# A selective scan with its products moved off VectorE: B in transposed layout on ScalarE, C on GpSimd, the sum over states by TensorE transposes

## The chip, the core and the metric

The kernel runs on one core of one Trainium2 chip. A core has a matrix engine (TensorE, PE; its weight loads are listed apart as PEld), three engines for elementwise work (VectorE, DVE; ScalarE, ACT; GpSimd, POOL), a queue engine that issues transfers (SyncE, SP), an on-chip memory of 128 partitions (SBUF) and a small accumulator memory of eight banks of 128 x 512 float32 (PSUM), which TensorE writes and which GpSimd is not used on here. Each engine runs its own list of instructions in order, and semaphores make one engine wait for another. The metric is the device time of one execution in microseconds; lower is better.

## What is computed

The input is x of shape 4 x 32 x 32 x 256: 4 batches of 1024 tokens with 256 channels. Everything is float32. Layer 0 is a convolution with a selective scan, layer 1 an attention and a mixture of 16 experts. The change touches layer 0 alone:

```python
x = _layernorm(src, ln1_g, ln1_b) @ w_in + b_in           # 256 -> Dn = 512 channels
x = gelu(depthwise_conv3x3(x) + conv_b).reshape(B, L, Dn)  # L = 1024 tokens
dt_raw, Bm, Cm = split(x @ w_x, [R, R + N])                # R = 16, N = 64 states
dt = softplus(dt_raw @ w_dt + dt_bias)
A = -exp(A_log)                                            # Dn x N
def step(h, inp):                                          # h: B x Dn x N
    dA = exp(dtt[:, :, None] * A)
    h = dA * h + (dtt * xt)[:, :, None] * Bt[:, None, :]
    y = einsum('bdn,bn->bd', h, Ct)
...
y = ys + x * D_skip
out = _layernorm(y, ln2_g, ln2_b) @ w_out + b_out
return src + out
```

For each of 4 batches, 512 channels and 64 states there is a recurrence over 1024 tokens. Its input is dt x B, its decay is exp(dt A), and what it gives is multiplied by C and summed over the 64 states.

## The kernel before

The program is written in Python that unrolls all loops. A tile framework takes the instructions that the Python code traces, orders them for each engine by a priority list of its own, gives out buffers from pools (`bufs=3` means three buffers that are used in turn) and puts in the semaphores. So the order on an engine is not always that of the source, and a tile can only be written when the last reader of the buffer's earlier content is done.

The residual stream `t_all` stays in SBUF, tokens on partitions. Layer 0 goes batch by batch (`for b in range(NB)`). The 512 channels are held as DK = 4 blocks of 128 partitions, and tokens run along the free dimension, in NHALF = 2 halves of 512 (one PSUM bank).

- Front part (L184 to L265): layernorm of the tokens, transposes (`transposed`, L107), the projection in (L201), the convolution as nine products with diagonal matrices (L214), gelu, the projection to B, C and dt (L229, L234; B and C stand in `bct`, states on partitions, tokens along the row), and the softplus in steps on ScalarE, VectorE and GpSimd (L247 to L265), which gives `dt` and `dtx` = dt x. Its tiles z, e, ln and u have two buffers each.
- Scan part (L275 to L331): for each half of the tokens and each of the 64 states n. `drive` (L288) spreads row n of B over all partitions with a product (L282), ScalarE copies it to SBUF as `bb` (L292), and VectorE and GpSimd each multiply two of the four blocks of `dtx` with it (L295), which gives `dbx`. ScalarE makes the decay `da` in PSUM (L307), VectorE runs the scan of each block (L310), 512 tokens in one instruction. Row n of C is spread into PSUM as `p_c`, VectorE multiplies the four blocks of h with it in one instruction (L318), and TensorE adds the product `hc` into four banks `y`, channels on partitions, by multiplying with the identity (L322). The last column of h is kept in `last` as the start of the second half.
- Rear part (L327 to L371): y + D x (L328), layernorm over the channels by means of products with a matrix of 1/512 (L341, L349), the projection out (L365) and the residual sum (L370, L371).

Layer 1 (attention, router, experts; lines from 373 on) is the same before and after. A float32 product is two passes on TensorE, a transpose one.

Of the kernel before, what the change touches and what calls it, by code (L numbers as in the profile page):

```python
# [18 lines left out]
def over_middle(ap, n):  # L19
    """[P, F] read n times: [P, n, F]."""  # L20
    return ap.unsqueeze(1).to_broadcast([ap.shape[0], n, ap.shape[1]])


def over_last(ap, n):
    """[P, F] with each element read n times: [P, F, n]."""
    return ap.unsqueeze(2).to_broadcast([ap.shape[0], ap.shape[1], n])
# [3 lines left out]
def conv_ssm_attn_moe_kernel(ctx: ExitStack, tc: tile.TileContext, a: dict, out: bass.AP):  # L30
# [24 lines left out]
    # The residual stream, tokens on partitions: token (g * 128 + p) is t_all[p, g].  # L55
# [14 lines left out]
    def load_rows(name, k, n, pool):  # L70
        """A [k * 128, n] matrix, rows on partitions."""
        t = pool.tile([P, k, n], F32, name=name.lower() + "_sb")
        nc.sync.dma_start(out=t, in_=a[name].rearrange("(k p) n -> p k n", p=P))
        return t

    def load_column(name, k, pool, lo=0):
        """A vector along partitions, in k blocks of 128."""
        t = pool.tile([P, k], F32, name=f"{name.lower()}_col")
        with nc.allow_non_contiguous_dma(reason="small vectors, once"):
            nc.scalar.dma_start(  # L80
                out=t, in_=a[name][lo : lo + k * P].rearrange("(k p) -> p k", p=P)
            )
        return t

    def load_bcast(name, n, pool):
        """A vector along the free dimension, on all partitions."""
# [4 lines left out]
    def token_layernorm(pool, dst, src, n, tag):  # L91
        """dst = (src - mean) / sqrt(var + 1e-5) over the last dimension of [P, n, C]."""
# [14 lines left out]
    def transposed(psum, src, n, evacuate, tag):  # L107
        """[P tokens, n, C] -> evacuate(ck, half, [P channels, 512 tokens] in PSUM)."""
# [14 lines left out]
    # ------------------------------------------------------------------  # L123
    # Layer 0: conv + selective scan, channels on partitions
    # ------------------------------------------------------------------
    with ExitStack() as l0:
# [28 lines left out]
        # One diagonal matrix for each tap and channel block: the depthwise conv on TensorE.  # L155
# [6 lines left out]
        # 1 / DN everywhere: a product with it is the mean over channels, on all partitions.  # L162
        avg = w0.tile([P, P], F32, name="avg")
        nc.vector.memset(avg, 1.0 / DN)
        # The padded conv inputs; their borders stay zero.
# [6 lines left out]
        acts = l0.enter_context(tc.tile_pool(name="acts0", bufs=1))  # L172

        for b in range(NB):
# [3 lines left out]
            dtx = acts.tile([P, DK, L], F32, name="dtx")  # L178
            bct = acts.tile([P, L], F32, name="bct")

            with tc.tile_pool(name=f"ps_a{b}", bufs=4, space=PSUM) as ps_a, tc.tile_pool(
                name=f"pre{b}", bufs=1
            ) as pre:
                xn = pre.tile([P, NT, C], F32, name="xn")  # L184
                token_layernorm(pre, xn, tb, NT, "ln1")
                xT = pre.tile([P, CK, L], F32, name="xT")

                def put_x(ck, half, ps):
                    nc.scalar.activation(
                        xT[:, ck, blk(half)], ps, AF.Identity,  # L190
                        bias=b1[:, ck : ck + 1], scale=g1[:, ck : ck + 1],
                    )

                transposed(ps_a, xn, NT, put_x, "ps")

                for m in range(DK):
                    pad = pads[m % 2]
                    for half in range(NHALF):
                        ps = ps_a.tile([P, BANK], F32, name="ps_in", tag="ps")
                        for ck in range(CK):  # L200
                            nc.tensor.matmul(  # L201
                                ps, w_in[:, ck, blk(m, P)], xT[:, ck, blk(half)],
                                start=(ck == 0), stop=(ck == CK - 1),
                            )
                        nc.vector.tensor_scalar(  # L205
                            pad[:, 1 + half * ROWS : 1 + (half + 1) * ROWS, 1 : 1 + WW],
                            ps.rearrange("p (h w) -> p h w", w=WW),
                            b_in[:, m : m + 1], None, ALU.add,
                        )
                    for half in range(NHALF):  # L210
                        ps = ps_a.tile([P, BANK], F32, name="ps_conv", tag="psc", bufs=2)
                        for k in range(9):
                            i, j = divmod(k, 3)
                            nc.tensor.matmul(  # L214
                                ps.rearrange("p (h w) -> p h w", w=WW),
                                diag[:, m, k, :],
                                pad[:, half * ROWS + i : (half + 1) * ROWS + i, j : j + WW],
                                start=(k == 0), stop=(k == 8),
                            )
                        nc.scalar.activation(  # L220
                            xg[:, m, blk(half)], ps, AF.Gelu_apprx_tanh, bias=cb[:, m : m + 1]
                        )

                dtr = pre.tile([R, L], F32, name="dtr")
                for half in range(NHALF):
                    psb = ps_a.tile([P, BANK], F32, name="ps_bc", tag="ps")
                    psd = ps_a.tile([P, BANK], F32, name="ps_dtr", tag="ps")
                    for m in range(DK):
                        nc.tensor.matmul(  # L229
                            psb, w_x[:, m, R:], xg[:, m, blk(half)],  # L230
                            start=(m == 0), stop=(m == DK - 1),
                        )
                    for m in range(DK):
                        nc.tensor.matmul(  # L234
                            psd[:R, :], w_x[:, m, :R], xg[:, m, blk(half)],
                            start=(m == 0), stop=(m == DK - 1),
                        )
                    nc.scalar.copy(dtr[:, blk(half)], psd[:R, :])
                    nc.vector.tensor_copy(bct[:, blk(half)], psb)

                # softplus(z) = max(z, 0) + log1p(e), e = exp(-|z|). With u = fl(1 + e),
                # log1p(e) = ln(u) + (e - (u - 1)) to within a rounding.
                for m in range(DK):
                    z = pre.tile([P, L], F32, name="z", tag="z", bufs=2)
                    for half in range(NHALF):
                        ps = ps_a.tile([P, BANK], F32, name="ps_dt", tag="ps")
                        nc.tensor.matmul(  # L247
                            ps, w_dt[:, blk(m, P)], dtr[:, blk(half)], start=True, stop=True
                        )
                        nc.vector.tensor_scalar(  # L250
                            z[:, blk(half)], ps, dtb[:, m : m + 1], None, ALU.add
                        )
                    e = pre.tile([P, L], F32, name="e", tag="e", bufs=2)
                    nc.scalar.activation(e, z, AF.Abs)
                    nc.scalar.activation(e, e, AF.Exp, scale=-1.0)
                    ln = pre.tile([P, L], F32, name="ln", tag="ln", bufs=2)
                    nc.scalar.activation(ln, e, AF.Ln, bias=1.0)
                    u = pre.tile([P, L], F32, name="u", tag="u", bufs=2)
                    nc.vector.tensor_scalar(u, e, 1.0, 1.0, ALU.add, ALU.subtract)
                    nc.gpsimd.tensor_tensor(u, e, u, ALU.subtract)  # L260
                    nc.gpsimd.tensor_tensor(u, u, ln, ALU.add)
                    nc.vector.scalar_tensor_tensor(
                        dt[:, m, :], z, 0.0, u, ALU.max, ALU.add
                    )
                    nc.gpsimd.tensor_tensor(dtx[:, m, :], dt[:, m, :], xg[:, m, :], ALU.mult)  # L265

            # h[d, n, t] = exp(dt[d, t] A[d, n]) h[d, n, t - 1] + dt[d, t] x[d, t] B[n, t];
            # y[d, t] = sum over n of h[d, n, t] C[n, t]: d on partitions, t along the scan.
            # TensorE copies the rows of B and C to all partitions and adds up over n.
            yt = dt  # L270
            last = acts.tile([P, NS, DK], F32, name="last")
            with tc.tile_pool(name=f"ps_y{b}", bufs=1, space=PSUM) as ps_y, tc.tile_pool(
                name=f"ps_e{b}", bufs=2, space=PSUM
            ) as ps_e, tc.tile_pool(name=f"scan{b}", bufs=2) as scanp:
                for seg in range(NHALF):  # L275
                    y = [
                        ps_y.tile([P, BANK], F32, name=f"y{m}", tag=f"y{m}") for m in range(DK)
# [372 lines left out]
```

## Time and profile before

| what | value |
|---|---|
| time, median of 3 runs | 7884.99 us (7884.57 to 7887.02) |
| span of the profiled execution | 7886.5 us |
| batch 0: first scan to last C product | 164.8 to 1196.1 us |
| batch 1 | 1383.7 to 2414.9 us |
| batch 2 | 2602.6 to 3633.7 us |
| batch 3 | 3821.0 to 4852.5 us |
| layer 1 | from about 4897 us on |
| busy: PE / DVE / ACT / POOL | 6606.9 / 5134.6 / 2326.0 / 1381.8 us |

The profiled execution's time is its span, as nothing lies around it that the runs' times would show. In the rows of a profile, "L310 DVE TENSOR_TENSOR_SCAN h<-da,dbx 128x512" is an instruction of line 310 on VectorE that writes tile h from da and dbx; behind it stand the count, the busy time in all, the mean of one in ns, and behind the bar the idle time of the engine just before such instructions, with what ended it. In timeline rows the first two numbers are start and length in us; rows of equal instructions that follow each other are merged, with their count. Instructions that follow each other without a gap overlap a little in these records, so the step from one start to the next is the better measure of a steady cost.

### The profile page before, as it was taken

The page shows a single profiled execution, that of the slowest core. Times are in us where ns is not written, and L with a number is a line of the kernel's source. Part 1 is how long each engine was busy: PE and PEld are TensorE (multiplying, and loading weights), DVE is VectorE, ACT ScalarE, POOL GpSimd, SP SyncE. Part 2 cuts the span into 40 slices and gives each one's busy share as a digit, 9 for nine tenths or more (in the row PEclk, how much of TensorE's full clock was granted, in tenths as well). Part 3 has the DMA queues.
Part 4 walks back from the last instruction along what each step waited for, and adds up shares of the span by engine and source line. Part 5 has one row for each costly group of instructions (what it writes and reads, how often), then busy time and mean ns, then how long its engine had stood idle before and what let it go on. Part 6 is the DMA issues. An engine that isn't in the chain of part 4 may idle for free.

```text
span 7886.5 us, 46169 instructions
## 1 busy us (share of the span) xinstructions
PE 6606.9 (84%) x16768; PEld 3257.8 (41%) x16768; DVE 5134.6 (65%) x5222; ACT 2326.0 (29%) x3771; POOL 1381.8 (18%) x631
## 2 busy tenths in 40 slices
PE   6777777777778677777777777999999999999999
PEld 2222323222233222323232233655555555555555
DVE  3999993999994899995799999542222222222222
ACT  2444442444442444442444443211111111111111
POOL 2222221322220423221322221000000000000000
PEclk8999998899999899999899999889999999999999
DMA  1000000000000000000000000000000000000000
GB/s 30 0 0 0 0 0 0 0 0 0 0 0 0 0 0 0 0 0 0 0 0 0 0 0 24 1 0 8 8 16 8 8 8 8 16 8 8 8 8 22
DMA packets 37701, 39.78 MB, mean 5 GB/s; under 512 B 10704, under 2 KB 28624, under 8 KB 37472
## 3 DMA queue, kind: packets, MB, share of 16 engines
q1 hardware_dynamic: 28240, 36.13, 1.5%
q8 instruction: 131, 2.15, 0.1%
q10 hardware_dynamic: 9232, 0.70, 0.1%
q14 instruction: 98, 0.80, 0.0%
HBM read 32.63 MB, written 4.19 MB: 5 GB/s over the span
## 4 chain that ended last, share of the span: by engine, by line
DVE 45%; PE 43%; issue 9%; POOL 1%; ACT 1%; DMA 0%; ACTq 0%; SPq 0%; DVEq 0%; POOLq 0%
DVE h L310 26%; PE p L591 22%; PE pf L602 11%; DVE hc L318 10%; DVE dbx L295 8%; PE ps_conv L214 3%; PE po L365 1%; PE ps_in L201 1%; PE ps_t L113 1%; PE pqk L426 1%; PE pkv L474 0%; PE y L322 0%; POOL u L260 0%; PE ps_dtr L234 0%; PE ps_bc L229 0%
## 5 line engine op out<-in xcount | busy, mean ns | idle before, releaser
L322 PE MATMUL y<-hc,ident 128*128 128x512 f32 x4096 | 2106.8, 663 | 12.8 <-DVE hc L318 12.8
L307 ACT ACTIVATE da<-dt,l_conv_a_log_sb 128x512 f32<-128x512 f32 x2048 | 1415.1, 691 | 2025.9 <-DVE h L310 2012.0
L591 PE MATMUL p<-xfT,w 128*128 128x512 f32 x4096 | 1781.0, 593 | 0.3 <-DVE pr L539 0.3
L295 POOL TENSOR_TENSOR dbx<-dtx,bb 128x1024 f32<-128x1024 f32 x512 | 1217.8, 2379 | 2825.6 <-DVE h L310 2820.5
L282 PE MATMUL p_c<-bct,ident 128*128 128x512 f32 x1024 | 630.0, 700 | 997.2 <-DVE hc L318 997.1
L322 PEld LDWEIGHTS y<-hc,ident 128*128 128x128 f32 x4096 | 884.1, 216 | 1198.1 <-issue 1179.0
L597 DVE TENSOR_TENSOR hT<-s,p 128x512 f32<-128x512 f32 x512 | 352.0, 688 | 1437.3 <-PE p L591 1436.6
L310 DVE TENSOR_TENSOR_SCAN h<-da,last,dbx 128x512 f32<-128x512 f32 x1024 | 1264.8, 1287 | 0.0
L310 DVE TENSOR_TENSOR_SCAN h<-da,dbx 128x512 f32<-128x512 f32 x1024 | 1193.4, 1207 | 0.1
L318 DVE TENSOR_TENSOR hc<-h,p_c 128x2048 f32<-128x2048 f32 x512 | 1169.8, 2285 | 28.1 <-DVE h L310 1.8
L591 PEld LDWEIGHTS p<-xfT,w 128*128 128x128 f32 x4096 | 778.9, 190 | 926.7 <-issue 919.8
L596 ACT ACTIVATE s<-p 128x512 f32<-128x512 f32 x512 | 305.7, 597 | 2324.3 <-PE p L591 2324.3
L602 PE MATMUL pf<-w,hT 128*128 128x256 f32 x4096 | 904.9, 379 | 0.0
L602 PEld LDWEIGHTS pf<-w,hT 128*128 128x128 f32 x4096 | 778.2, 190 | 160.4 <-issue 61.2
L282 PEld LDWEIGHTS p_c<-bct,ident 128*128 128x128 f32 x1024 | 156.7, 191 | 1422.2 <-DVE hc L318 1412.0
L282 PE MATMUL p_b<-bct,ident 128*128 128x512 f32 x1024 | 549.7, 619 | 143.1 <-ACT bb L292 92.4
L606 DVE SCALAR_TENSOR_TENSOR t_all<-pf,disp,t_all 128x256 f32<-128x256 f32 x512 | 247.8, 484 | 601.3 <-PE pf L602 601.3
L295 DVE TENSOR_TENSOR dbx<-dtx,bb 128x1024 f32<-128x1024 f32 x512 | 634.8, 1240 | 3.1 <-ACT bb L292 3.1
L292 ACT COPY bb<-p_b 128x512 f32<-128x512 f32 x512 | 299.5, 585 | 294.7 <-DVE dbx L295 246.4
L282 PEld LDWEIGHTS p_b<-bct,ident 128*128 128x128 f32 x1024 | 195.6, 194 | 417.5 <-ACT bb L292 246.0
L214 PE MATMUL ps_conv<-pad,diag 128*128 128x512 f32 x576 | 249.8, 592 | 0.0
L205 DVE TENSOR_SCALAR pad<-ps_in,l_conv_b_in_col 128x512 f32<-128x512 f32 x32 | 24.1, 753 | 229.9 <-PE ps_in L201 229.8
(143 smaller groups left out, 2077.9 us busy)
## 6 DMA issues: line engine op xcount, KB each, us to landing
w<-in_L_ffn_w_dram SPq DMA_DIRECT2D x48, 512.0 KB, 3.9
t_all<-in_x_dram SPq DMA_DIRECT2D x4, 1024.0 KB, 7.6
out_dram<-t_all SPq DMA_DIRECT2D x8, 512.0 KB, 2.9
l_attn_w_qkv_sb<-in_L_attn_W_qkv_dram SPq DMA_DIRECT2D x1, 768.0 KB, 6.6
l_conv_w_in_sb<-in_L_conv_w_in_dram SPq DMA_DIRECT2D x1, 512.0 KB, 11.4
l_conv_w_out_sb<-in_L_conv_w_out_dram SPq DMA_DIRECT2D x1, 512.0 KB, 7.4
l_attn_b_qkv_row<-in_L_attn_b_qkv_dram ACTq DMA_DIRECT2D x1, 384.0 KB, 5.3
l_conv_w_x_sb<-in_L_conv_w_x_dram SPq DMA_DIRECT2D x1, 288.0 KB, 9.9
```

The costliest lines, as they stand in the source:

```text
L214: nc.tensor.matmul(ps.rearrange("p (h w) -> p h w", w=WW), diag[:, m, k, :], pad[:, half * ROWS + i : (half + 1) * ROWS + i, j : j + WW], ...
L282: nc.tensor.matmul(ps, ident[:, row : row + 1].to_broadcast([P, P]), bct[:, blk(seg)], start=True, stop=True,)
L292: nc.scalar.copy(bb, pb)
L295: eng.tensor_tensor(dbx[:, lo:hi, :], dtx[:, lo:hi, blk(seg)], over_middle(bb, hi - lo), ALU.mult,)
L307: nc.scalar.activation(da, dt[:, m, blk(seg)], AF.Exp, scale=A[:, m, n : n + 1])
L310: nc.vector.tensor_tensor_scan(h[:, m, :], da, dbx[:, m, :], 0.0 if seg == 0 else last[:, n, m : m + 1], ALU.mult, ALU.add,)
L318: nc.vector.tensor_tensor(hc, h, over_middle(pc, DK), ALU.mult)
L322: nc.tensor.matmul(y[m], ident, hc[:, m, :], start=(n == 0), stop=(n == NS - 1))
L591: nc.tensor.matmul(ps, w[:, ck, blk(hk, P)], xfT[:, ck, blk(tbk)], start=(ck == 0), stop=(ck == CK - 1),)
L596: nc.scalar.activation(s, p1, AF.Silu)
L597: nc.vector.tensor_tensor(hT[:, hk, :], s, p2, ALU.mult)
L602: nc.tensor.matmul(pf, hT[:, hk, blk(j, P)], w3[:, hk, :], start=(hk == 0), stop=(hk == HK - 1),)
```

## The change

In the scan, four things are laid out in another way.

1. **dt x B.** `dtx` is transposed once a batch on TensorE, into `dtxT` with tokens on partitions and channels along the row, and so is B, into `bT`. For a state n, B is then one number per partition, and ScalarE multiplies a token tile of 128 tokens x 512 channels with it as the `scale` of an activation (L323, four a state). TensorE transposes the 16 blocks of 128 x 128 back into PSUM (L330), from where the scan reads them. The decay `da` now goes to SBUF (L332, four buffers).
2. **C.** The C rows are written to a scratch tensor `cd` in the device memory once a batch (L245), and for each state one row is loaded onto all 128 partitions (L318, three buffers). GpSimd multiplies h with it, two blocks at a time (L346). It also makes the copies into `last` (L344).
3. **The sum over n.** Instead of adding up `hc` with channels on partitions, `turned_sum` (L304) adds transposes of its 128 x 128 blocks into the four banks `y`, which now have tokens on partitions. Their first summand is the transpose of D x, for which GpSimd multiplies `xg` with D in place (L294).
4. **After the sum,** the second layernorm works on tokens on partitions with VectorE's statistics instructions (L357 to L363), and its result is transposed back for the projection out. This now runs after each half, before the scans of the next half in VectorE's order.

VectorE keeps the scans and has neither product any more. All pools of layer 0 are opened once rather than once a batch; the tiles of the front part have one buffer each and share them with others (z with xn, e with xT, bct with ln, dtx with u). PSUM is four banks for `y` and four that everything else takes in turn (`bank()`).

```diff
         acts = l0.enter_context(tc.tile_pool(name="acts0", bufs=1))
+        pre = l0.enter_context(tc.tile_pool(name="pre", bufs=1))
+        scanp = l0.enter_context(tc.tile_pool(name="scan", bufs=2))
+        ps_y = l0.enter_context(tc.tile_pool(name="ps_y", bufs=1, space=PSUM))
+        ps_w = l0.enter_context(tc.tile_pool(name="ps_w", bufs=4, space=PSUM))
+        dram0 = l0.enter_context(tc.tile_pool(name="dram0", bufs=2, space=bass.MemoryType.DRAM))
+
+        def bank():
+            return ps_w.tile([P, BANK], F32, name="ps", tag="ps")
...
+            nc.sync.dma_start(out=cd, in_=bct[NS:, :])
+            for half in range(NHALF):
+                ps = bank()
+                for j in range(TPB):
+                    nc.tensor.transpose(
+                        ps[:, blk(j, P)], bct[:, blk(half * TPB + j, P)], ident
+                    )
+                nc.scalar.copy(
+                    bT[:, half * TPB : (half + 1) * TPB, :],
+                    ps.rearrange("p (j n) -> p j n", n=P)[:, :, :NS],
+                )
...
+                dtx = pre.tile([P, L], F32, name="dtx", tag="u")
+                nc.gpsimd.tensor_tensor(dtx, dt[:, m, :], xg[:, m, :], ALU.mult)
+                for half in range(NHALF):
+                    ps = bank()
+                    for j in range(TPB):
+                        nc.tensor.transpose(
+                            ps[:, blk(j, P)], dtx[:, blk(half * TPB + j, P)], ident
+                        )
+                    nc.scalar.copy(
+                        dtxT[:, half * TPB : (half + 1) * TPB, blk(m, P)],
+                        ps.rearrange("p (j d) -> p j d", d=P),
+                    )
+
+                nc.gpsimd.tensor_scalar(
+                    xg[:, m, :], xg[:, m, :], dsk[:, m : m + 1], None, ALU.mult
+                )
...
-                        for eng, lo, hi in ((nc.gpsimd, DK // 2, DK), (nc.vector, 0, DK // 2)):
-                            eng.tensor_tensor(
-                                dbx[:, lo:hi, :], dtx[:, lo:hi, blk(seg)],
-                                over_middle(bb, hi - lo), ALU.mult,
-                            )
...
-                        nc.vector.tensor_tensor(hc, h, over_middle(pc, DK), ALU.mult)
-                        if n + 1 < NS:
-                            pc = spread(NS + n + 1, "c")
-                        for m in range(DK):
-                            nc.tensor.matmul(
-                                y[m], ident, hc[:, m, :], start=(n == 0), stop=(n == NS - 1)
-                            )
...
+            def turned_sum(y, src, first, stop):
+                for j in range(TPB):
+                    for m in range(DK):
+                        nc.tensor.matmul(
+                            y[j][:, blk(m, P)], src(m, j), ident, is_transpose=True,
+                            start=first and m == 0, stop=stop and m == DK - 1,
+                            skip_group_check=True,
+                        )
+
+            for seg in range(NHALF):
+                y = [ps_y.tile([P, DN], F32, name=f"y{j}", tag=f"y{j}") for j in range(TPB)]
+                turned_sum(y, lambda m, j: xg[:, m, blk(seg * TPB + j, P)], True, False)
+                for n in range(NS):
+                    cb_n = scanp.tile([P, BANK], F32, name="cb_n", bufs=3)
+                    nc.sync.dma_start(out=cb_n, in_=cd[n, blk(seg)].partition_broadcast(P))
+                    bx = []
+                    for j in range(TPB):
+                        i = seg * TPB + j
+                        bx.append(scanp.tile([P, DN], F32, name="bx", bufs=6))
+                        nc.scalar.activation(
+                            bx[j], dtxT[:, i, :], AF.Copy, scale=bT[:, i, n : n + 1]
+                        )
+                    hcs = []
+                    for m in range(DK):
+                        dbx = bank()
+                        for j in range(TPB):
+                            nc.tensor.transpose(dbx[:, blk(j, P)], bx[j][:, blk(m, P)], ident)
+                        da = scanp.tile([P, BANK], F32, name="da", bufs=4)
+                        nc.scalar.activation(
+                            da, dt[:, m, blk(seg)], AF.Exp, scale=A[:, m, n : n + 1]
+                        )
+                        if m % 2 == 0:
+                            h = scanp.tile([P, 2, BANK], F32, name="h", bufs=3)
+                        nc.vector.tensor_tensor_scan(
+                            h[:, m % 2, :], da, dbx,
+                            0.0 if seg == 0 else last[:, n, m : m + 1],
+                            ALU.mult, ALU.add,
+                        )
+                        if m % 2:
+                            if seg + 1 < NHALF:
+                                nc.gpsimd.tensor_copy(last[:, n, m - 1 : m + 1], h[:, :, BANK - 1])
+                            hc = scanp.tile([P, 2, BANK], F32, name="hc", bufs=3)
+                            nc.gpsimd.tensor_tensor(hc, h, over_middle(cb_n, 2), ALU.mult)
+                            hcs.append(hc)
+                    turned_sum(
+                        y, lambda m, j: hcs[m // 2][:, m % 2, blk(j, P)], False, n == NS - 1
+                    )
+
+
+                for j in range(TPB):
+                    i = seg * TPB + j
+                    st = pre.tile([P, 6], F32, name="st2", bufs=2)
+                    mv = pre.tile([P, 2], F32, name="mv2", bufs=2)
+                    nc.vector.bn_stats(st, y[j])
+                    nc.vector.bn_aggr(mv, st)
+                    rs = pre.tile([P, 1], F32, name="rs2", bufs=2)
+                    nc.scalar.activation(rs, mv[:, 1:2], AF.Sqrt, bias=eps5)
+                    nc.vector.reciprocal(rs, rs)
+                    yn = pre.tile([P, DN], F32, name="yn", tag="ln")
+                    nc.vector.tensor_scalar(yn, y[j], mv[:, 0:1], rs, ALU.subtract, ALU.mult)
+                    ps = bank()
+                    for m in range(DK):
+                        nc.tensor.transpose(ps[:, blk(m, P)], yn[:, blk(m, P)], ident)
+                    yT = pre.tile([P, DK, P], F32, name="yT", tag="u")
...
```

The order that the framework gives the instructions of the changed program on each engine can be read from the program as it is built, before it runs; the prediction uses that.

## The prediction

> **What bounds the kernel now.** I read the page's busy shares and slices first, then the chain, then the busy time of the four scan stages, then the groups, then the timeline of one state.
>
> ```profile
> PE 6606.9 (84%) x16768; PEld 3257.8 (41%) x16768; DVE 5134.6 (65%) x5222; ACT 2326.0 (29%) x3771; POOL 1381.8 (18%) x631
> ...
> DVE  3999993999994899995799999542222222222222
> ...
> DVE 45%; PE 43%; issue 9%; POOL 1%; ACT 1%; DMA 0%; ACTq 0%; SPq 0%; DVEq 0%; POOLq 0%
> ```
>
> PE's 84% misleads: VectorE (DVE) is full in four blocks of the first 60% of the span, with PE full only behind them. These are the four batches' scan stages:
>
> ```profile
> 164.80:1196.10 1031.30, 770.44 (x1522) 306.23 (x1522) 1023.83 (x772) 433.02 (x701) 303.46 (x128) 0.92 0.00 0
> 1383.70:2414.90 1031.20, 771.40 (x1522) 306.71 (x1522) 1023.66 (x771) 433.03 (x701) 303.53 (x128) 0.91 0.00 0
> ```
>
> Columns: length; busy time of PE, PEld, DVE, ACT, POOL with counts; granted clock. DVE is busy 1024 of 1031 us; all four stages sum to 4125 us, 512 rounds (64 states, two halves of the sequence, four batches) of 8.06. The groups inside, and one round:
>
> ```profile
> L295 POOL TENSOR_TENSOR dbx<-dtx,bb 128x1024 f32<-128x1024 f32 x512 | 1217.8, 2379 | 2825.6 <-DVE h L310 2820.5
> L310 DVE TENSOR_TENSOR_SCAN h<-da,last,dbx 128x512 f32<-128x512 f32 x1024 | 1264.8, 1287 | 0.0
> L310 DVE TENSOR_TENSOR_SCAN h<-da,dbx 128x512 f32<-128x512 f32 x1024 | 1193.4, 1207 | 0.1
> L318 DVE TENSOR_TENSOR hc<-h,p_c 128x2048 f32<-128x2048 f32 x512 | 1169.8, 2285 | 28.1 <-DVE h L310 1.8
> ```
>
> ```profile
> 670.26 2.29 DVE L318 TENSOR_TENSOR hc<-h,p_c 128x2048 f32<-128x2048 f32 x1
> 672.47 2.33 DVE L310 TENSOR_TENSOR_SCAN h<-da,dbx 128x512 f32<-128x512 f32 x2
> 674.71 1.20 DVE L295 TENSOR_TENSOR dbx<-dtx,bb 128x1024 f32<-128x1024 f32 x1
> 675.83 2.33 DVE L310 TENSOR_TENSOR_SCAN h<-da,dbx 128x512 f32<-128x512 f32 x2
> 678.26 2.29 DVE L318 TENSOR_TENSOR hc<-h,p_c 128x2048 f32<-128x2048 f32 x1
> ```
>
> No gap: 4 scans, a B product and a C product follow each other. Back to back, scans start 1.125 us apart in the first half, 1.185 in the second.
>
> **The change, by engine.** DVE loses the two products and keeps 4 scans: 4.6 to 4.8 us a round. ACT gets 4 B products (128x512, one scale per partition) instead of the 0.585 copy; with the 4 exponentials, 8 x 0.63 (start to start, exponential to copy, 1390.94 to 1391.57) to 8 x 0.72 (the two-column activations of L357, 8 in 5.75): 5.0 to 5.8. GpSimd swaps one 128x1024 product for two, and in the first half two tiny copies: 2 x 2.35 = 4.7, plus 2 x 0.15 (between its 0.10 memset and ACT's 0.20 for the same copy). PE gets 32 one-pass transposes for 12 matmul passes. Their price depends on the clock:
>
> ```profile
> 1245.88 4.04 PE L113 MATMUL ps_t<-ident,xn 128*128 128x128 f32 x16 [5.94 <-DVE xn L102]
> 1249.71 4.65 PE L201 MATMUL ps_in<-xT,l_conv_w_in_sb 128*128 128x512 f32 x8
> ```
>
> ```profile
> 4987.41 0.60 PE L113 MATMUL ps_t<-ident,xh 128*128 128x128 f32 x4
> 4987.85 1.02 PE L426 MATMUL pqk<-l_attn_w_qkv_sb,xhT 128*128 128x512 f32 x2
> ```
>
> At clock 0.5, 16 take 3.83 us to the next matmul, 0.239 each; at 1.0, 4 take 0.44, 0.110 each (one's own duration: 0.42 and 0.27). So 32 cost 3.5 to 7.6. The 512 row loads for C (256 KB each) go on SP's queue, which holds nothing else in that stage; the nearest rows, broadcast loads of 128 and 384 KB, land after 5.3 to 6.9 us, and three buffers let them be issued over two rounds ahead: nothing. If that cover went, up to 7 us a round.
>
> Were every engine free to run ahead, the round would be the slowest sum, 5.0 to 5.8. **The order on PE forbids it.** PE's queue as built, in the first half: 8 sums of state n's channel blocks 0,1; three transposes for n+1; 8 sums of blocks 2,3; and only then the fourth transpose that the first scan of n+1 needs (in all but 1 or 2 of the 64 rounds). The sums wait for GpSimd, so nothing of n+1 can be scanned before GpSimd and PE have finished n. In the second half, 24 of 64 rounds have the first scan's tile complete before the sums; there only the second scan waits.
>
> Hops between engines are 0.05 to 0.08 (a scan ended at 646.14 and GpSimd began at 646.22; a C product at 1006.56 and PE at 1006.61). From T, the end of n's last scan, first half: scan 1 ended at T-2.25; hop 0.08, copy 0.15, 0.07, product 2.35: T+0.40; 0.05, copy 0.15, 0.07, product 2.35: T+3.02 (second half, without copies: T+2.48). Hop 0.06, 8 sums (0.88 warm, 1.91 cold), a last transpose to its end (0.27, 0.42), hop 0.06. Then 4 scans, 3 x 1.125 + 1.204 = 4.58 (second half 4.84; 3.66 where three remain).
>
> - first half: 8.87 warm, 10.05 cold; 256 rounds
> - second half, all four behind: 8.59, 9.77; 160 rounds
> - second half, three behind: 7.41, 8.59; 96 rounds
>
> Sum: 4356 warm, 4961 cold, against 4125: +231 and +836. The relief of DVE (3.5 us a round) is more than taken back by a gap of 3.7 to 5.5 between rounds.
>
> **Which clock.** Warm, PE would end the transposes behind the sums at T+5.4 and start again at the next T+0.46: 3.9 us of idling each round, longer than the longest wait (3.5) for p_c now, whose stage has 0.92. The record changes in steps of 3.41 us, and a step that is mostly idle is followed by 0.50. Cold, PE is busy 7.6 of 10 us, so it warms up again, but after the critical sums. I take 4/5 of the way to cold: +715; both ends stay.
>
> [...]
>
> ```profile
> 3685.53:3688.94 3.41, 3.41 (x12) 2.41 (x11) 0.06 (x1) 2.77 (x5) 0.00 (x0) 0.50 0.00 0
> 3688.94:3692.36 3.42, 3.42 (x9) 1.52 (x8) 1.36 (x2) 0.74 (x1) 0.00 (x0) 1.00 0.00 0
> 1384.95:1388.36 3.41, 2.07 (x2) 0.50 (x2) 3.41 (x3) 2.50 (x4) 3.03 (x2) 0.50 0.00 0
> 1388.36:1391.77 3.41, 2.08 (x2) 0.50 (x2) 3.41 (x3) 1.51 (x4) 2.95 (x2) 0.50 0.01 2
> ```
>
> The first step, eight transposes (from 3685.53 on) and matmuls, released the clock; the last two, with two 512-column passes each and nothing else, did not.
>
> **Outside the scans.** Between the halves of a batch, DVE's order puts the layernorm and projection of four token tiles before the next scan: about 13 us for the first (0.82 statistics, 1.3 table load, 0.75 normalizing, 1.1 transposes, 1.6 four activations, 2 to 3.4 projection, 0.42 + 0.72 adding, hops) and 4 for each further one, whose buffers are single; 28, less the 5 that a round's gap already has: +23 x 4 = 92; before, the seam cost some 5 us. Softplus: with single buffers each block's chain z to dt (1.5 + 1.05 + 1.28 + 1.06 + 0.69 + 2 x 2.4 + 1.25) runs alone, 12 x 4 + 10 against 46: +12 x 4 = 48. The next batch's layernorm is done during the scan: -9 x 3. The batch's own tail is 30 instead of 45: -60. Sum +53; taken as +60, between -40 and +150.
>
> The profiled execution's span is 7886.5 and the runs shown are 7884.6 to 7887.0, so nothing lies around the span; it stands 1.5 above the median 7885.0 (0.02%). 7886.5 + 715 + 60 = **8660**.
>
> **Rivals.**
> - Warm throughout: the gap is there but PE keeps its clock. For it: transposes count. Against: 3.9 us idle. 7886.5 + 231 + 60 = 8180.
> - Faster: the queues' order does not bind, and the round is ACT's sum, 5.4: 512 x 5.4 = 2765, 7886.5 - 1360 + 60 = 6590. It decides if the gap between n's last scan and the next scan falls under 8.06 - 4.7 - 0.1 (the outside, by round) = 3.2 us. For it: the sums of all engines. Against: the order as built, and PE has one queue.
> - Cold throughout, and everything else at its long end: 7886.5 + 836 + 150, and 0.1 more of hops a round (51): 8920. For it: cold PE is busy 7.6 of 10 us and yet late each time. Against: a full step of transposes releases the clock.
> - The change does not do what it says: DVE would keep a product; the order as built has only scans there, so I give it nothing.
>
> **How the numbers follow.** Mixed clock 0.50; warm 0.17; cold and longer 0.20; faster 0.11; 0.02 that the gap lands on the break-even. The range reaches from warm (8180, less the 70 that the outside may be lower) to cold: 8110 to 8920. Faster (over 0.2%, about what a measurement of this kernel can tell) 0.11, same 0.02, slower 0.87.
>
> **What would show it.** The profile after: DVE busy near 2900 us in all, its scans 2450 with 1900 us idle before them, released by PE's transposes; in each round GpSimd's second product, the sums, one transpose, then four scans in a row; clock in the scan stage 0.55 to 0.75 (0.50 if cold throughout, 1.0 by the warm rival). I am wrong if the first scan of a round starts while GpSimd is still at the state before, or if a row load ends the wait.

## The result

The changed kernel takes 8529.7 us (median of 4 runs, 8528.4 to 8531.7) against 7884.9 before: a ratio of 1.082 (95% interval 1.080 to 1.083), 8.2% slower. The prediction was 8660, with a range of 8110 to 8920. The profiled execution has a span of 8529.9.

From the page of the changed kernel: busy time of each engine, the slices of VectorE (DVE) and of TensorE's granted clock, and the groups of the scan part (count | busy, mean ns | idle time before them and what ended most of it).

```profile
PE 6558.9 (77%) x27296; PEld 4745.8 (56%) x27296; DVE 3406.6 (40%) x4269; ACT 3275.7 (38%) x5220; POOL 2674.3 (31%) x1671
...
DVE  2444553444555244455334455564222222222222
...
PEclk8767778666877776787866688788999999999999
...
L346 POOL TENSOR_TENSOR hc<-h,cb_n 128x1024 f32<-128x1024 f32 x1024 | 2413.7, 2357 | 1044.5 <-issue 1030.7
...
L337 DVE TENSOR_TENSOR_SCAN h<-da,ps 128x512 f32<-128x512 f32 x1024 | 1166.8, 1201 | 1255.9 <-PE ps L330 1255.9
L337 DVE TENSOR_TENSOR_SCAN h<-da,last,ps 128x512 f32<-128x512 f32 x1024 | 1233.4, 1262 | 1010.2 <-PE ps L330 998.0
```

VectorE lost 1728 us of work, and its row shows it: half empty in the stretches where it stood at 9 before. No engine is full there instead. The scans themselves are as long as before, but 2266 us of idling now stand in front of them, nearly all ended by PE's transposes (L330). The next view is the first half and the second half of batch 0, from first to last scan, with the busy time of PE, PEld, DVE, ACT and POOL, then the granted clock, the share of the DMA engines and GB/s.

```profile
201.00:802.00 601.00, 389.63 (x2019) 349.71 (x2017) 291.60 (x257) 323.12 (x509) 312.98 (x254) 0.69 0.09 28
824.30:1386.80 562.50, 359.79 (x2028) 314.84 (x2026) 308.27 (x257) 326.82 (x503) 299.85 (x128) 0.81 0.09 29
```

Each engine is busy for 49% to 65% of the time in these halves: they take turns. One round of the first half, from the timeline (start, length in us; in brackets the idle time and what ended it):

```profile
415.10 4.55 DVE L337 TENSOR_TENSOR_SCAN h<-da,ps 128x512 f32<-128x512 f32 x4 [4.44 <-PE ps L330]
...
417.50 0.19 POOL L344 COPY last<-h 128x2 f32<-128x2 f32 x1 [4.06 <-DVE h L337]
417.64 2.35 POOL L346 TENSOR_TENSOR hc<-h,cb_n 128x1024 f32<-128x1024 f32 x1
...
419.93 0.18 POOL L344 COPY last<-h 128x2 f32<-128x2 f32 x1
...
420.07 2.36 POOL L346 TENSOR_TENSOR hc<-h,cb_n 128x1024 f32<-128x1024 f32 x1
...
421.00 0.84 PE L330 MATMUL ps<-ident,bx 128*128 128x128 f32 x3
...
422.48 1.97 PE L307 MATMUL y<-ident,hc 128*128 128x128 f32 x8 [0.64 <-POOL hc L346]
...
424.24 1.06 PE L330 MATMUL ps<-ident,bx 128*128 128x128 f32 x4
424.80 1.22 DVE L337 TENSOR_TENSOR_SCAN h<-da,ps 128x512 f32<-128x512 f32 x1 [5.14 <-PE ps L330]
```

Four scans end at 419.65. GpSimd's second product ends at 422.43, the eight sums that wait for it take until 424.24, the transpose that the next scan needs comes behind them, and the scan starts at 424.80: 9.70 us after the last round's start.

Where the 643 us lie, by the starts and ends of the scans in the two profiled executions:

| stretch | before | after | difference |
|---|---|---|---|
| start to first scan | 164.8 | 201.0 | +36 |
| scans, first to last of the 8 half batches | 4107.3 | 4651.9 | +545 |
| between the halves of a batch, 4 | 9.2 | 89.5 | +80 |
| between batches, 3 | 568.8 | 574.9 | +6 |
| after the last scan | 3036.3 | 3012.6 | -24 |
| span | 7886.5 | 8529.9 | +643 |

### The profile page after: what moved, and what is told of

Same layout as the page of the kernel before. It is cut to its first block, busy times and chain, and to the rows that moved or that the text cites. A ratio compares the mean times of both kernels' runs of the same rounds, so it can differ in the third digit from the quotient of the medians.

```text
span 8529.9 us, 72895 instructions
## 1 busy us (share of the span) xinstructions
PE 6558.9 (77%) x27296; PEld 4745.8 (56%) x27296; DVE 3406.6 (40%) x4269; ACT 3275.7 (38%) x5220; POOL 2674.3 (31%) x1671
## 5 line engine op out<-in xcount | busy, mean ns | idle before, releaser
L346 POOL TENSOR_TENSOR hc<-h,cb_n 128x1024 f32<-128x1024 f32 x1024 | 2413.7, 2357 | 1044.5 <-issue 1030.7
L307 PE MATMUL y<-ident,hc 128*128 128x128 f32 x8192 | 1686.7, 373 | 1285.8 <-POOL hc L346 1283.0
L307 PEld LDWEIGHTS y<-ident,hc 128*128 128x128 f32 x8192 | 1367.7, 195 | 1512.7 <-POOL hc L346 1512.3
L323 ACT ACTIVATE bx<-dtxT,bT 128x512 f32<-128x512 f32 x2048 | 1357.7, 710 | 1836.8 <-PE ps L330 1836.6
L330 PE MATMUL ps<-ident,bx 128*128 128x128 f32 x8192 | 1593.6, 343 | 385.8 <-DVE h L337 371.5
L337 DVE TENSOR_TENSOR_SCAN h<-da,ps 128x512 f32<-128x512 f32 x1024 | 1166.8, 1201 | 1255.9 <-PE ps L330 1255.9
L337 DVE TENSOR_TENSOR_SCAN h<-da,last,ps 128x512 f32<-128x512 f32 x1024 | 1233.4, 1262 | 1010.2 <-PE ps L330 998.0
L330 PEld LDWEIGHTS ps<-ident,bx 128*128 128x128 f32 x8192 | 1339.5, 183 | 506.5 <-DVE h L337 371.6
L332 ACT ACTIVATE da<-dt,l_conv_a_log_sb 128x512 f32<-128x512 f32 x2048 | 1371.8, 712 | 239.1 <-DVE h L337 174.0
L344 POOL COPY last<-h 128x2 f32<-128x2 f32 x512 | 96.2, 188 | 1170.9 <-DVE h L337 1170.9
L217 PE MATMUL ps<-pad,diag 128*128 128x512 f32 x576 | 249.8, 592 | 0.0
L217 PEld LDWEIGHTS ps<-pad,diag 128*128 128x128 f32 x576 | 108.8, 189 | 138.4 <-issue 138.4
```

The source lines that it names most:

```text
L217: nc.tensor.matmul(ps.rearrange("p (h w) -> p h w", w=WW), diag[:, m, k, :], pad[:, half * ROWS + i : (half + 1) * ROWS + i, j : j + WW], ...
L307: nc.tensor.matmul(y[j][:, blk(m, P)], src(m, j), ident, is_transpose=True, start=first and m == 0, stop=stop and m == DK - 1, skip_group_ ...
L323: nc.scalar.activation(bx[j], dtxT[:, i, :], AF.Copy, scale=bT[:, i, n : n + 1])
L330: nc.tensor.transpose(dbx[:, blk(j, P)], bx[j][:, blk(m, P)], ident)
L332: nc.scalar.activation(da, dt[:, m, blk(seg)], AF.Exp, scale=A[:, m, n : n + 1])
L337: nc.vector.tensor_tensor_scan(h[:, m % 2, :], da, dbx, 0.0 if seg == 0 else last[:, n, m : m + 1], ALU.mult, ALU.add,)
```

## The experiments

Four accounts stood against each other. **S**: PE's one queue has the sums of state n in front of a transpose that the first scan of n+1 needs, so VectorE, GpSimd and PE work in series; the half clock makes PE's part longer (0.22 us a transpose). **C**: 32 transposes at half clock (0.22 each, 7 us a round) are the bound by themselves. **G**: GpSimd's two products are the bound. **D**: GpSimd waits for the row loads of C, as the "issue" in its row above could mean.

### All transposes of the next state before the sums of this one

The work is the same; each sum is placed in PE's queue behind the last transpose of the next state.

```diff
+                            turn = nc.tensor.transpose(dbx[:, blk(j, P)], bx[j][:, blk(m, P)], ident)
...
-                    turned_sum(
-                        y, lambda m, j: hcs[m // 2][:, m % 2, blk(j, P)], False, n == NS - 1
-                    )
+                    if n:
+                        with tc.issue_after(turn.ins):
+                            turned_sum(
+                                y, lambda m, j, t=held: t[m // 2][:, m % 2, blk(j, P)], False, False
+                            )
+                    held = hcs
+                turned_sum(
+                    y, lambda m, j, t=held: t[m // 2][:, m % 2, blk(j, P)], False, True
+                )
```

> The sums of state n stand on PE behind all 16 transposes of n+1; the same instructions otherwise. Theory S (PE's one queue makes DVE, GpSimd and PE take turns): DVE no longer waits for GpSimd's second product. The transposes go token tile by token tile, so a round's first scan waits for the bank of the scan before and then for 16 transposes: gap 16 x 0.11 + 0.27 + 0.1 = 2.1 us, round 6.7 to 6.95, 512 x 6.85 = 3507 against 4652 now: 7390 us if PE stays warm, up to 8200 if it is cold (each gap 1.8 longer). Rival C (the transposes' own time at half clock is the bound, 32 x 0.22 = 7.0 us, and their number is unchanged) and rival G (GpSimd's two products): about 8530, unchanged.

Measured: 7032.3 us, a ratio of 0.892 (0.890 to 0.893) to the kernel before. Order alone takes 1497 us off the changed kernel. C and G, which left it at 8530, fall. In the two traces VectorE, ScalarE and GpSimd run the same instructions in the same order; PE's order alone is another. The rounds take 6.06 us in the first half and 6.30 in the second. One of them, from the timeline:

```profile
401.29 4.55 DVE L337 TENSOR_TENSOR_SCAN h<-da,ps 128x512 f32<-128x512 f32 x4 [1.50 <-PE ps L330]
...
404.21 0.38 PE L330 MATMUL ps<-ident,bx 128*128 128x128 f32 x2
...
404.79 0.33 PE L330 MATMUL ps<-ident,bx 128*128 128x128 f32 x1 [0.20 <-DVE h L337]
...
405.90 1.64 PE L330 MATMUL ps<-ident,bx 128*128 128x128 f32 x13 [0.78 <-DVE h L337]
...
407.35 4.55 DVE L337 TENSOR_TENSOR_SCAN h<-da,ps 128x512 f32<-128x512 f32 x4 [1.50 <-PE ps L330]
```

A gap of 1.50 is left, and it is again one of order. With the sums moved, PE goes through the 16 transposes token tile by token tile: one for each of four banks, then the next four. The fourth needs the bank that the round's last scan has just freed (it ends at 405.84, PE goes on at 405.90), and 12 transposes stand behind it, three of which the next first scan needs. The last of these three is the ninth of the 12. So ten transposes lie in the gap, where the expectation put 16: the gap is 1.50 instead of 2.1, and the time 7032 instead of the 7390 expected with a warm clock.

### Transposes block by block

The same, but PE finishes one channel block, and so one bank, before it begins the next. Transposes and sums are chained in this order (`queued` places an instruction behind the one named).

```diff
+                            pe = queued(
+                                pe, nc.tensor.transpose,
+                                dbx[:, blk(j, P)], bx[j][:, blk(m, P)], ident,
+                            )
...
+                    if n:
+                        pe = sums(y, held, pe, False)
+                    held = hcs
+                sums(y, held, pe, True)
```

> As the run before, but with the transposes channel block by channel block and the sums in two groups of 8, in this order on PE. Theory S: the first scan's tile of n+1 is ready before n's last scan ends, no gap is left on DVE, and the round is the slowest engine's sum: ACT 8 x 0.66 = 5.3 us (DVE 4.6 to 4.75, GpSimd 4.7 to 5.1, PE 3.5 warm). 512 x 5.35 = 2740 against 4652: 6620 us, 6550 to 6800, with PE's clock near 1.0 in the scan stage (3.5 of 5.35 busy). Rivals C and G: about 8530.

Measured: 6389.5 us (6388.4 to 6391.6), a ratio of 0.810 (0.809 to 0.811): 19% faster than the kernel before, with the same instructions as the slower one. VectorE and GpSimd run them in the same order as there, and so does ScalarE but for one exchange of two at the start of each batch. One round from its timeline, then three pieces of it of 3.41 us:

```profile
404.20 2.55 ACT L354 ACTIVATE da<-dt,l_conv_a_log_sb 128x512 f32<-128x512 f32 x4
...
404.86 1.91 PE L318 MATMUL ps<-ident,bx 128*128 128x128 f32 x16
405.59 4.55 DVE L359 TENSOR_TENSOR_SCAN h<-da,ps 128x512 f32<-128x512 f32 x4 [0.33 <-ACT da L354]
...
406.42 2.35 POOL L368 TENSOR_TENSOR hc<-h,cb_n 128x1024 f32<-128x1024 f32 x1
...
406.60 1.04 PE L318 MATMUL y<-ident,hc 128*128 128x128 f32 x8
406.65 2.54 ACT L342 ACTIVATE bx<-dtxT,bT 128x512 f32<-128x512 f32 x4
```

```profile
400.00:403.41 3.41, 2.75 (x26) 2.52 (x24) 3.05 (x4) 3.41 (x6) 3.41 (x3) 1.00 0.27 80
403.41:406.82 3.41, 2.89 (x26) 2.90 (x27) 3.08 (x4) 3.41 (x7) 3.41 (x5) 1.00 0.34 77
406.82:410.23 3.41, 2.22 (x21) 1.99 (x20) 3.33 (x3) 3.41 (x6) 3.41 (x3) 1.00 0.08 21
```

A round is 4.91 us in both halves; 512 of them make 2503 us of scanning where the kernel before has 4107. In these pieces ScalarE and GpSimd are busy without a break, and the clock is at 1.00, with PE running nothing but transposes here. VectorE waits 0.33 us a round in the first half and 0.1 in the second. ScalarE's step is 0.61 us (eight in 4.91), below the 0.63 to 0.72 that I had worked with, and with it the time lies below the 6550 to 6800 expected.

### The sums first, all of them

The other direction: PE's queue holds 16 transposes of n, then 16 sums of n, then the transposes of n+1, so that four transposes stand between the sums and the scan in every round. The transposed B products take turns in three banks; the fourth is free and is used by the next kernel.

```diff
-        ps_w = l0.enter_context(tc.tile_pool(name="ps_w", bufs=4, space=PSUM))
+        ps_w = l0.enter_context(tc.tile_pool(name="ps_w", bufs=3, space=PSUM))
...
+                    pe = sums(y, hcs, pe, n == NS - 1)
```

> The order of the source on PE, forced: all 16 sums of n before any transpose of n+1; and PSUM has three banks in turn instead of four, with one kept for the next run. Theory S: every round now has the full chain, and four transposes after the sums instead of one: gap 4.44 + 0.33 = 4.8 warm, 5.14 + 0.66 = 5.8 cold, round 9.3 to 10.5; 512 x 10.0 = 5120: 9000 us, 8850 to 9150. Rival C: 8530 plus or minus 60, as the number of transposes is the same.

Measured: 9098.5 us, a ratio of 1.154 (1.151 to 1.156), clock 0.67 in both halves of batch 0, rounds of 10.3 us. Later transposes, longer rounds, as S has it. ScalarE's order is another here too, so this kernel doesn't differ by PE's order alone. But the rows below show the longer chain: from the first transpose behind the sums to the scan it is 1.17 us (416.25 to 417.42), against 0.56 in the changed kernel (424.24 to 424.80).

### The same with products added that nobody needs

Four plain products of 512 columns a round are put into PE's queue where it waits for GpSimd: three before the first eight sums, one before the last eight.

```diff
+                    if m == 2:
+                        before = queued(
+                            before, nc.tensor.matmul, spare, ident, dt[:, 0, blk(seg)],
+                            start=True, stop=True,
+                        )
...
+                    for _ in range(3):
+                        pe = queued(
+                            pe, nc.tensor.matmul, spare, ident, dt[:, 0, blk(seg)],
+                            start=True, stop=True,
+                        )
```

> As the run before, with four plain products (8 passes of 512 columns) a round added on PE into the spare bank, read by nobody: three before the first 8 sums, one before the last 8, where PE waits for GpSimd. Theory S with the clock as the second part: PE has no longer an idle stretch that halves the clock, the sums run at 0.11 us each, and the added work lies in waits: gap 4.8, round 9.2 to 9.5, 512 x 9.35 = 4790: 300 us less than the run before, with a clock of 0.95 to 1.0 in the scan stage. If the clock does not matter: no change against the run before. Rival C: PE is the bound, so 8 x 0.43 to 8 x 0.87 a round more: 1780 us or more on top.

Measured: 8460.7 us, a ratio of 1.073 to the kernel before, 638 us less than without the filler. From the timelines, the kernel without it and the kernel with it, from the last eight sums of a round to the next scan:

```profile
414.49 1.97 PE L322 MATMUL y<-ident,hc 128*128 128x128 f32 x8 [1.34 <-POOL hc L372]
...
416.25 3.62 PE L322 MATMUL ps<-ident,bx 128*128 128x128 f32 x16
417.42 4.55 DVE L363 TENSOR_TENSOR_SCAN h<-da,ps 128x512 f32<-128x512 f32 x4 [5.75 <-PE ps L322]
```

```profile
406.81 1.10 PE L322 MATMUL y<-ident,hc 128*128 128x128 f32 x8 [0.49 <-POOL hc L377]
...
407.74 1.47 PE L322 MATMUL ps<-ident,bx 128*128 128x128 f32 x12
408.45 4.55 DVE L368 TENSOR_TENSOR_SCAN h<-da,ps 128x512 f32<-128x512 f32 x4 [4.48 <-PE ps L322]
```

From the sums' start to the scan it is 2.93 us without and 1.64 with the filler; 512 times the difference of 1.29 is 660. My 300 was too low by half: twelve transposes on this path at 0.22 instead of 0.11 are 1.3 us, and I had allowed for the clock being back up at the sums in part of the rounds; in the round without the filler it is not (eight sums in 1.76 us, 414.49 to 416.25, against 0.93 with it, 406.81 to 407.74). The first half of batch 0 without and with the filler, with the columns of the stretches above:

```profile
200.90:854.30 653.40, 419.15 (x2020) 369.32 (x2020) 291.50 (x258) 327.86 (x512) 312.54 (x254) 0.67 0.09 26
200.70:774.30 573.60, 482.63 (x2530) 301.24 (x2530) 291.49 (x258) 328.68 (x512) 313.26 (x254) 1.00 0.10 30
```

The direction is what counts: PE got 1.9 ms more work and the kernel became 7% faster, so in this order the half clock is a part of the loss, and one that comes from PE's waiting. No run fills the waits of the changed kernel itself, so the clock's share of its 645 us stays open.

### One C row for all states

```diff
+                cb_n = scanp.tile([P, BANK], F32, name="cb_n", bufs=3)
+                nc.sync.dma_start(out=cb_n, in_=cd[0, blk(seg)].partition_broadcast(P))
                 for n in range(NS):
-                    cb_n = scanp.tile([P, BANK], F32, name="cb_n", bufs=3)
-                    nc.sync.dma_start(out=cb_n, in_=cd[n, blk(seg)].partition_broadcast(P))
```

> The changed kernel, but one C row is loaded per half of a batch and used for all 64 states (the other 504 row loads and their values are left out). By S (PE's queue order makes the engines take turns) the row loads are hidden: 8530 within 15 us. By D (GpSimd waits for the row loads, as the 1031 us of idling that its products' row puts down to 'issue' could mean) up to 1000 us go: 7530 to 8300.

Measured: 8536.1 us, a ratio of 1.082 (1.081 to 1.084), the same as the changed kernel. D falls. GpSimd's row on the page shows what "issue" stood for:

```profile
L346 POOL TENSOR_TENSOR hc<-h,cb_n 128x1024 f32<-128x1024 f32 x1024 | 2412.0, 2357 | 1053.0 <-DVE h L337 1044.7
```

With a single load there is no second wait in front of the product, and the same idling (1053 against 1045 us) is now put down to the scan. So GpSimd had not been waiting for the loads.

### Half a C product, with the sums first and with the better order

GpSimd multiplies half of the columns; the sums read each of these twice, so PE's work and order stay.

```diff
-                            nc.gpsimd.tensor_tensor(hc, h, over_middle(cb_n, 2), ALU.mult)
+                            nc.gpsimd.tensor_tensor(
+                                hc[:, :, : BANK // 2], h[:, :, : BANK // 2],
+                                over_middle(cb_n[:, : BANK // 2], 2), ALU.mult,
+                            )
```

In the kernel with the sums first and the filler:

> The kernel with the sums first and the filler (clock at 1.0, 8461), but GpSimd multiplies only half of the columns by C, and the sums take each of these twice, so that PE's work and order stay (the product of the other columns is left out). By S GpSimd's second product stands in series with the sums and the scans: it ends about 1.5 us earlier after the last scan in the first half (0.08 + 0.05 + 0.15 + 0.07 + 1.2 against 3.02) and 1.2 in the second; 256 x 1.5 + 256 x 1.2 = 690 off: 7770, between 7650 and 8000. If GpSimd is off the path, 8460 within 30.

In the kernel with the block-by-block order:

> The same halving of GpSimd's product in the kernel with the block-by-block order (6389.5, rounds of 4.9 us). There GpSimd (44 us idle before its products) and ScalarE (64 us before its exponentials) are both nearly full. If GpSimd sets the round, it falls to VectorE's four scans, about 4.6 and 4.85: some 90 less, 6300. If ScalarE's eight instructions of 0.61 set it, nothing changes: 6390 within 25. By S in its plain form (GpSimd in series with the scans) 690 would go: 5700; I expect the second.

Measured: 7850.3 us for the first, 610 less than its whole product (690 expected), and 6374.8 for the second (ratio 0.808, 0.807 to 0.809), 15 less. The rounds of the first went from 9.03 to 7.72 us and from 8.99 to 7.90. One of them, with half products:

```profile
400.65 4.55 DVE L368 TENSOR_TENSOR_SCAN h<-da,ps 128x512 f32<-128x512 f32 x4 [3.16 <-PE ps L322]
...
405.41 1.28 POOL L377 TENSOR_TENSOR hc<-h,cb_n 128x512 f32<-128x512 f32 x1
...
406.74 1.09 PE L322 MATMUL y<-ident,hc 128*128 128x128 f32 x8
```

GpSimd's second product ends 1.49 after the last scan (405.20 to 406.69), about the 1.55 forecast. With whole products it is 2.79 (403.97 to 406.76 in that kernel's trace), where I had 3.02. That makes up some 45 of the 80 us between 690 and 610; in the second half it is the half product, which takes 1.28 where I had put 1.2. The rounds of the second kernel stayed at 4.90. Its products' row on the page, then the first half of batch 0, and behind it the two halves of batch 0 with whole products:

```profile
L368 POOL TENSOR_TENSOR hc<-h,cb_n 128x512 f32<-128x512 f32 x1024 | 1306.7, 1276 | 600.6 <-issue 311.9
```

```profile
200.00:513.00 313.00, 264.41 (x2029) 225.32 (x2027) 291.44 (x257) 311.41 (x508) 180.30 (x256) 0.99 0.18 54
200.30:513.20 312.90, 235.51 (x2020) 219.34 (x2018) 291.39 (x257) 311.46 (x508) 310.48 (x254) 1.00 0.18 53
536.60:849.40 312.80, 252.49 (x2028) 220.50 (x2026) 306.29 (x257) 309.35 (x503) 301.76 (x128) 1.00 0.18 52
```

So the same saving is worth 610 us where GpSimd stands in series, and next to nothing where the queue lets the engines run beside each other. There ScalarE is the bound: it is busy 311 of 313 us while GpSimd falls from 310 to 180. The two profiled executions are 18 us apart: 10 of these lie between the halves of the batches (20.8 instead of 23.4 in batch 0), 4 between the batches and only 3 in the scans.

## Why the prediction was right, and where its sizes were off

**The queue.** The step on which all rested, that the fourth transpose behind the sums forbids running ahead, is shown by the two kernels that change PE's order alone: 8530 becomes 7032 and 6390, by nothing else than where sums and transposes stand in one queue. In the first half, 62 of the 63 gaps between rounds stand before the first scan, as the order says. In the second half the first scan comes early, with a second wait behind it, in 13 to 15 rounds of a half; I had 24 of 64.

**The gap, term by term** (first half, cold; the round shown above). GpSimd's second product ends 2.78 after the last scan; I had 3.02, because I put hops of 0.05 to 0.07 between GpSimd's own instructions, where the records overlap: copy, product, copy and product start at 417.50, 417.64, 419.93 and 420.07. The eight sums take 1.76 (422.48 to 424.24); I had 1.91, from 0.239 a transpose, where these take 0.22. The last transpose and the hops take 0.61; I had 0.54. Together 5.15 instead of 5.47, and a cold round of 9.70 instead of 10.05. The rounds that I called warm take 8.98 instead of 8.87, since their sums begin before the clock is back: in the round ahead of the one shown the last eight start at 413.49, the clock is at 0.50 until 414.10, and they take 1.20 (to 414.69) where I had 0.88.

**The clock.** It goes back and forth as worked out, at 0.69 to 0.70 in the first halves, but is higher in the second, 0.81 to 0.82, where I had said 0.55 to 0.75 for all. Of the way from warm to cold I took 4/5. By the measured rounds of 8.98 and 9.70, the first half's mean of 9.48 is at 0.69 of it; in the second half the mean of 8.8 is at little over half the way between my own ends (8.15 and 9.33 as the mean of its two kinds of round). With the shorter terms this is the miss in the scans: 4840 us forecast (4125 + 715), 4652 measured (of the 4125, 18 lie between the halves and behind the last scans, which the 4107 and 4652 of the table leave out). It is the largest mis-sized term of the sum.

**Outside the scans** I had +60 and it is +98. Of the difference, 20 us is bookkeeping: the forecast counts the gap behind the first half's last round among the rounds ("less the 5 that a round's gap already has"), the table counts it between the halves. Counted alike, the miss in the scans is 20 smaller. The stretch between two halves takes 22.4 us rather than 28: 13.2 to the first token tile's last addition, as put, then 3.05 for each further one instead of 4 (814.76, 817.80, 820.91, 823.95). The first batch's front is 36 longer where I had 12 for it, and the tails and the next batches' fronts together give back 18 where I had 51. What is left of these misses opposes the one in the scans, so the total is off by 130 us, 1.5%.

**What was to be seen** in the profile: the scans' busy time is 2400 (2450 forecast) and the idle time before them 2266 (1900 forecast), released by PE's transposes. The 1900 was a slip: the forecast's own rounds, 4840, less 2450 leave 2390. DVE's busy time is 3407, not "near 2900"; that figure was a slip, since 5135 less the C products (1170) and the B products (512 x 1.2 = 614) is 3351. The range has one more: its low end takes 70 off for the outside, where going from +60 to -40 is 100, so it should have been 8080. And a run's time is 1.8 us longer than its span (8531.7 against 8529.9 in the profiled execution), so not quite nothing lies around it.

**The rivals.** "Faster" was priced at 6590 by ScalarE's sum of 5.4 a round. The mechanism is the one that the block-by-block kernel has, at 4.91 a round and 6390. It needed the gap to fall under 3.2 us, and in the changed kernel it is 5.1 in most rounds of the first half. "Warm throughout" (8180) did not come, and the nearest thing to it, the filler, lowers a kernel of another order by 638.

## What to carry to other kernels

The sum of each engine's work says what a round could be; the order within each in-order queue says what it is. So when work moves from a full engine to others, follow one queue across the boundary of a round, above all the one that both makes an input (transposes for n+1) and takes in a result (sums of n): whatever waits for the slowest result goes behind everything that the next round needs, and inputs are finished one consumer at a time. TensorE, waiting in such a chain, lost its clock here too (0.69 to 0.70 in the first halves of the changed kernel, 0.67 in batch 0 with the sums first), which lengthened the chain (with the sums first, eight sums took 1.76 us, and 0.93 with the filler, at 1.00). With the order mended the clock followed: over the whole program it is 0.96 in the two better orders, against 0.83 in the changed kernel, and in the block-by-block order 1.00 in the scans of batch 0.

## What the runs showed of the hardware

**Transposes kept the clock here.** Steps of 3.41 us in the changed kernel in which PE runs only transposes (the sums over states are transposes too), with the same columns as the stretches above:

```profile
403.86:407.27 3.41, 3.41 (x18) 3.41 (x18) 1.16 (x2) 0.00 (x0) 0.00 (x0) 0.50 0.27 77
407.27:410.68 3.41, 0.71 (x6) 0.47 (x5) 3.39 (x4) 3.04 (x5) 2.17 (x2) 1.00 0.00 0
410.68:414.10 3.42, 3.05 (x14) 2.81 (x15) 0.00 (x0) 1.97 (x4) 2.76 (x3) 0.50 0.00 0
```

The step full of transposes (PE busy for 3.41 us, clock 0.50) is followed by one at 1.00, and this one, with PE busy for 0.71 us, by one at 0.50. In the block-by-block kernel PE has nothing but transposes in the scans, and the clock is at 1.00 in both halves of batch 0 and 0.99 in the first half of batch 1.

**Work that nobody needs paid here.** 2048 extra products (4096 passes), busy for 1930 us on PE, took 638 us off a kernel in which PE waits: the clock went from 0.67 to 1.00 in both halves of batch 0, and the twelve transposes in the path of a round became as much shorter as the round.

**"issue" hid a wait that is known.** 1031 us of GpSimd's idling stood under it, and with the row loads gone the same time stood under the scans. The label alone is no evidence for a transfer being late.
